# A conditional layer in 64x64 quarters whose tiles are turned by ScalarE's transposes, and products of zeros at both ends of an attention and feed-forward kernel

## The chip, the cores and the metric

The kernel runs on one core of one Trainium2 chip. The metric is the device time of one launch in microseconds (us), taken as the median of the runs shown. Below, PE is the matrix engine (TensorE), DVE the vector engine, ACT the scalar engine (ScalarE), POOL GpSimd, and SP the engine that issues most transfers. A phrase such as "L419" is line 419 of the kernel before.

## The reference

The input `x` has 64 batches of 64 channels and 1024 points in time. Two index vectors pick a weight set for each batch. Cut to what matters here:

```python
# x: (64, 64, 1024); itok_B_0_15: (64,) in 0..15; itok_B_0_7: (64,) in 0..7
W = weights[itok_B_0_15]                       # (64, 64, 64)
y = einsum('bct,bcd->bdt', x, W)               # the conditional layer
qkv = y @ attn_qkvw + attn_qkvb                # (.., 1024) @ (1024, 3072)
q, k, v = split into 32 heads of 32
probs = softmax(q @ k^T / sqrt(32))            # 64 x 64 per batch and head
x1 = x + (probs @ v) @ attn_ow + attn_ob
z = x1 @ W2^T + 2 * lora(x1, top-2 of 8 experts)
out = x1 + down(silu(gate(z)) * up(z))         # int8-quantized weights and activations
```

For every batch the conditional layer contracts over 64 channels with a 64x64 matrix of the batch's own. Its result has to stand with time on the partitions, because the projections to q, k and v contract over the 1024 points in time.

## The kernel before, in words

**Tiling.** Two batches of 64 channels make one tile of 128 rows and 1024 columns; there are 32 tiles, and four tiles are a block, so there are 8 blocks. In the attention stage (to about 1430 us) a block passes through four phases `c` = 0 to 3, one for every eight heads. All products of this stage are in f32.

**The conditional layer.** `load_x(b)` at the start of a block loads the four tiles of the next block (SP) and gathers their 64x64 weights (POOL). For each tile, the two weight matrices are copied into the diagonal blocks of a 128x128 matrix of zeros, `wbd` (L380, by POOL, in the first block by DVE). `conditional(b, tiles)` then makes eight products per tile with 128 columns of x as the stationary operand and `wbd` as the moving one (L355), which gives y with time on the partitions at once. Each half tile is copied out of PSUM by DVE (L361) or ACT (L363) into one of four quarters of the block, B11, B12, B21, B22 (rows by half of time, columns by half of the tokens; all are named yB in the profile). DVE makes four differences of quarters, T1 to T4 (L371, L376).

**Projections.** The projections use Winograd's scheme with seven products in place of eight, in the order 1, 6, 7, 5, 2, 4, 3. The first two use B11 and B22 and sums of them, the others T1 to T4. `rows_job` (L435) makes q or k of a phase: seven products of about 1.73 us; `values_job` (L462) makes v for two phases: seven of 3.45 us. After each product, its `rest` is run one product later: a copy by ACT (L406), a sum by DVE, or `put`, which writes a finished quarter: into `qT` for q, into `kbd` (keys with zeros between heads, four writes by ACT at L419 or by DVE at L421) for k, into `vbd` (L475) for v. The last two products of a job hold a PSUM bank of `ps_g` until they are put away, and the second product of the next job needs it.

**Scores, softmax, context.** `scores` (L498) multiplies q by kbd in 64x64 quadrants of PE, for two of four (half of heads, half of tokens) units at a time; a phase has two such groups, one at its start and one at its middle. DVE takes the maximum and subtracts it (L510, L511), ACT the exponential (L514), DVE the sum and the division (L520, L522). Then the probabilities are transposed without PE: ACT parts the f32 words into two int16 planes (`ph`, L528), SP issues a transposing transfer (`phT`, L533), and ACT joins the planes (`pT`, L540). `context` (L550) multiplies by vbd, ACT copies (L561) and issues the store of it (L562).

**The order of the work.** Nothing reorders the program: each engine works through its instructions in the order of emission. That order comes from a virtual clock. `run(cost, product, rest)` first calls everything whose due time in the list `due` has come, then emits a product, then the `rest` of the product before, and advances `now` by `cost`. `phase` puts the two score groups into `due` at 0 and at half of the phase's length, and hands the products in `fills` to `run`; each stage of softmax puts the next one into `due` with a fixed delay.

**The phases.** Phases 1 and 2 of a block hold q and k of the following phase. Phase 0 holds q, v for phases 2 and 3, and k. Phase 3 holds the whole conditional layer of the next block, then its v for phases 0 and 1, then its q and k. Phases 0 and 3 are the long ones. Phase 3 of the last block holds two products of the out-projection.

**Loads.** SP's queue carries x, the projections' weights (`wq`, `wk`: 1792 KB each, `wv`: seven of 512 KB), the transposes phT and some bfloat16 copies of later weights (`chores`), each at the place where it was emitted.

**The end.** The second stage (router, lora, quantized feed-forward) works through pairs of tiles. The end of its last pair is written out by hand: `gate_or_up` (L1491), `quant_b` (quantized rows transposed by a transfer or, with `by_pe`, by PE, L1481), and `down` (L1521), between DVE's work, which scales the results and finishes y (L1530).

Of the kernel before, what the change touches and what calls it, by code (L numbers as in the profile page):

```python
# [20 lines left out]
P = 128  # L21
# [161 lines left out]
def attention(tc, a, x_t, ctx_d, ident, dram, ps_g, KC, PB, NBLK, NCH, HPC, H, C, chores, early, op):  # L183
# [27 lines left out]
    with ExitStack() as ctx, ExitStack() as mid:  # L211
# [14 lines left out]
        xp = pool(early, "xp", 4)  # L226
# [12 lines left out]
        def load_x(b):  # L239
            tiles = []  # L240
            for j in range(PB):
                i = b * PB + j
                xt = xp.tile([P, H], F32, tag="x", name=f"x_{i}")
                if i == PB - 1:
                    held(xt[:, 0:1], tiles[0][0])
                nc.sync.dma_start(xt, x_t[i])
                wg = xp.tile([P, C], F32, tag="wg", name=f"wg_{i}")
                nc.gpsimd.indirect_dma_start(
                    out=wg[:, :],
                    out_offset=None,  # L250
                    in_=cw,
                    in_offset=bass.IndirectOffsetOnAxis(ap=idx[:, i:i + 1], axis=0),
                )
                tiles.append((xt, wg))
            return tiles

        def held(word, other):


            nc.scalar.copy(word, other[:, 0:1])  # L260
# [24 lines left out]
        def load_qk(b, wh, c, eng=None):  # L285
            t = w_qk[b, wh, c] = wp.tile([P, 7, KQ, P], F32, tag="wqk", name=f"w{wh}_{b}_{c}")
            if b == 0:
                if (wh, c) == ("q", 0):
                    held(t[:, SLOT["A11"], 0, 0:1], x_next[0][1])
                for key in RAW:  # L290
                    nc.sync.dma_start(t[:, SLOT[key], :, :], quarter(key, (0 if wh == "q" else H) + c * P, P))
                return sums(
                    eng or nc.vector, lambda key: t[:, SLOT[key], :, :], lambda: nc.gpsimd.dma_start(qk_d[wh, c], t)
                )
            nc.sync.dma_start(t, qk_d[wh, c])
# [21 lines left out]
        x_next = load_x(0)  # L317
# [7 lines left out]
        wbd = []  # L325
        for j in range(PB):
            t = w.tile([P, P], F32, tag=f"wbd{j}", name=f"wbd{j}")
            nc.vector.memset(t, 0.0)
            wbd.append(t)
# [12 lines left out]
        def conditional(b, tiles):  # L342

            def one(hf, j):
                key = f"B{hf + 1}{j // 2 + 1}"
                box = []

                def product():
                    xt = tiles[j][0]
                    if j % 2 == 0:  # L350
                        B[key] = yp.tile([P, KQ, HB], F32, tag=key, name=f"y{key}_{b}")
                    ps = ps_g.tile([P, 4, P], F32, tag="g", name=f"cond_{b}_{j}_{hf}")
                    for q in range(KQ):
                        k = hf * KQ + q
                        nc.tensor.matmul(ps[:, q, :], xt[:, k * P:(k + 1) * P], wbd[j], start=True, stop=True)  # L355
                    box.append(ps)

                def rest():
                    dst = B[key][:, :, (j % 2) * P:(j % 2 + 1) * P]
                    if j % 2 == 0:  # L360
                        nc.vector.tensor_copy(dst, box[0])  # L361
                    else:
                        nc.scalar.copy(dst, box[0])  # L363
                    if (hf, j) == (0, 3):
                        t_of("T1", "B12", "B11")
                    elif (hf, j) == (1, 3):
                        t_of("T2", "B22", "T1")
                        t_of("T3", "B22", "B12")
                    elif (hf, j) == (1, 1):
                        B["T4"] = B["B12"]  # L370
                        nc.vector.tensor_tensor(B["T4"], B["B21"], B["T2"], ALU.subtract)  # L371
                return 0.95, product, rest

            def t_of(key, x, y):
                B[key] = yp.tile([P, KQ, HB], F32, tag=key, name=f"{key}_{b}")
                nc.vector.tensor_tensor(B[key], B[x], B[y], ALU.subtract)  # L376

            for j, (_, wg) in enumerate(tiles):
                for r in range(2):
                    (nc.gpsimd if b else nc.vector).tensor_copy(wbd[j][halves[r], halves[r]], wg[halves[r], :])  # L380
            return [one(0, j) for j in range(PB)] + [one(1, j) for j in (2, 3, 0, 1)]
# [198 lines left out]
        def contexts(least=1):  # L580
            ready = sum(len(pTs) == 2 for *_, pTs in waiting)
            for n in range(ready if ready >= least else 0):
                context(*waiting.pop(0), 1.7 * n * (least - 1))

        def group(b, c, us):


            def begin():
                ps = scores(b, c, us)
                if behind:  # L590
                    behind.pop()()
                contexts(2)
                pTs = []
                waiting.append((b, c, us, pTs))
                for n, u in enumerate(us):
                    at(now + 1.7 * n, lambda n=n, u=u: first(u, ps[n], pTs))
                if b > 0:
                    at(now + 8.7, lambda: next(chores, None))
                    if c in (0, NP - 1):
                        at(now + 15, lambda: next(chores, None))  # L600
# [79 lines left out]
        for f in conditional(0, x_next):  # L680
            run(*f)
# [6 lines left out]
        for b in range(NBLK):  # L688
            if b + 1 < NBLK:
                x_next = load_x(b + 1)  # L690
            for c in range(NP):
                fills, length = [], None
                if c + 1 < NP:
                    fills += qk_fill(b, c + 1)
                    if c == 0:
                        fills[7:7] = v_fill(b, 1)
                        if b == 0:
                            for at_ in range(3, 7):
                                with_sums(fills, at_, v_raw, 1)
                elif b + 1 < NBLK:  # L700

                    fills += conditional(b + 1, x_next) + v_fill(b + 1, 0) + qk_fill(b + 1, 0)
# [305 lines left out]

class Winograd:
# [178 lines left out]
def second_stage(tc, a, out_t, xT_d, ident, ps_g, KC, NT, H, C, half, comb, op):  # L1188
# [12 lines left out]
    with ExitStack() as ctx:  # L1201
# [64 lines left out]

        ident_b = w.tile([P, P], BF16, tag="ident_b", name="ident_b")
# [200 lines left out]
        def quant_b(p, t, nm, by_pe=False):  # L1468
# [10 lines left out]
            ps = ps_g.tile([P, n // P, P], BF16, tag="g", name=f"qTp_{nm}_{p}_{t}")  # L1479
# [4 lines left out]
        def gate_or_up(p, t, nm):  # L1484
# [4 lines left out]
            ps = s["pgu", nm, t] = pool.tile([P, I], F32, tag=tag, name=f"p{nm}_{p}_{t}")  # L1489
            for k in range(KC):  # L1490
                nc.tensor.matmul(ps, qT[:, k, :], wt_b["w" + nm][:, k, :], start=(k == 0), stop=(k == KC - 1))  # L1491
# [22 lines left out]
        def down(p, t):  # L1514
            s = st[p]
            qT = s.pop(("qT", "i", t))
            for n in range(2):
                pool, tag = (ps_g, "g") if p == NPAIR - 1 else (ps_h, "h")
                ps = s["pd", t, n] = pool.tile([P, HH], F32, tag=tag, name=f"pd_{p}_{t}_{n}")
                for k in range(IC):  # L1520
# [136 lines left out]
        down(q, 0)  # L1657
# [5 lines left out]
        gate_or_up(p, 1, "g")  # L1663
        glu(p, 0)
        quant_b(q, 1, "i")
        gate_or_up(p, 1, "u")
# [8 lines left out]
        down(p, 0)  # L1675
        quant_b(p, 1, "i", True)
        result(q, 1, nc.gpsimd)
        result(p, 0, nc.gpsimd, nc.vector)
        down(p, 1)
# [55 lines left out]
```

## Time and profile before

| what | us |
|---|---|
| median of 3 runs | 2461.12 |
| lowest and highest run | 2460.36, 2464.75 |
| the profiled execution, its own time | 2458.5 |
| its span | 2456.7 |
| mean PE clock granted, of full speed | 0.998 |
| PE busy in the span | 2423.6 |
| DVE busy | 1532.9 |
| ACT busy | 953.2 |
| POOL busy | 362.9 |

The profile is one execution. Its time is the launch's, and the span runs from the first to the last instruction in the trace. "Busy" leaves out instructions that only wait, branch, or issue a transfer, so an engine can be held up for longer than its busy time says: the issue of a transposing transfer holds its engine too, and appears under SPq or ACTq, the sequencer of the engine. In a row of the timeline, the first number is the start and the second the length; what stands in brackets is the idle time before it and who ended it. In the waits, "A <- B: total, times, longest" says how long A's engine was idle until B's end released it.

### The profile page before, as it was taken

What the parts mean: (1) busy time and instruction counts of PE and PEld (TensorE: products, weight loads), DVE (VectorE), ACT (ScalarE), POOL (GpSimd) and SP (SyncE); (2) the same over time, 40 slices, a digit from 0 to 9 for tenths busy, and PEclk for the clock granted to TensorE, in tenths of its full rate; (3) what the DMA queues carried; (4) which work ended last, traced back from release to release, by engine and by line L of the source; (5) the groups of instructions that cost most, each with busy time, mean ns of one, the idle gap of its engine ahead of it and who ended that gap; (6) DMA issues with size and microseconds to landing.
All of it is one profiled execution on the core that took longest, in us unless ns stands there. A gap on an engine that the chain in (4) does not pass through costs nothing.

```text
span 2456.7 us, 34195 instructions
## 1 busy us (share of the span) xinstructions
PE 2423.6 (99%) x13194; PEld 1699.7 (69%) x13232; DVE 1532.9 (62%) x2955; ACT 953.2 (39%) x1304; POOL 362.9 (15%) x450
## 2 busy tenths in 40 slices
PE   8999999999999999999999999999999999999997
PEld 7888888888888888888888644444454545445452
DVE  4685585675664755745647633333367777878787
ACT  1343353342443443533434544344423333333333
POOL 5110001011122221210000243433200000000000
PEclk9999999999999999999999999999999999999999
DMA  8894767676677768766646588876744343434343
GB/s 275 286 268 150 219 198 234 189 213 211 199 204 248 202 193 249 206 204 180 176 142 218 175 266 247 268 239 218 235 140 80 88 80 77 89 70 92 74 118 75
DMA packets 419564, 448.07 MB, mean 182 GB/s; under 512 B 300737, under 2 KB 355010, under 8 KB 405698
## 3 DMA queue, kind: packets, MB, share of 16 engines
q1 hardware_dynamic: 388882, 379.21, 52.8%
q0 software_dynamic: 12080, 49.82, 7.6%
q10 hardware_dynamic: 18432, 16.79, 2.0%
q8 instruction: 106, 1.74, 0.3%
q14 instruction: 64, 0.52, 0.1%
HBM read 274.02 MB, written 100.66 MB: 153 GB/s over the span
## 4 chain that ended last, share of the span: by engine, by line
PE 95%; DVE 2%; ACT 1%; DMA 1%; issue 0%; ACTq 0%; SPq 0%; DVEq 0%
PE psva L462 5%; PE pska L435 5%; PE psvd L462 5%; PE psqa L435 5%; PE psvc L462 4%; PE psqc L435 4%; PE pskc L435 4%; PE psqd L435 4%; PE pskd L435 4%; PE pbc L1031 4%; PE pbd L1031 4%; PE pba L1031 4%; PE poa L1031 4%; PE pod L1031 4%; PE poc L1031 4%; PE s L498 3%
## 5 line engine op out<-in xcount | busy, mean ns | idle before, releaser
L540 ACT COPY pT<-phT 128x1024 int16<-128x1024 int16 x128 | 167.2, 1342 | 83.2 <-DMA phT<-ph 83.0
L514 ACT ACTIVATE prob<-prob 128x512 f32<-128x512 f32 x128 | 80.6, 630 | 258.6 <-DVE prob L511 232.4
L421 DVE SCALAR_TENSOR_TENSOR kbd<-pskd,bqkv,psku 32x256 f32<-32x256 f32 x256 | 123.2, 481 | 31.4 <-PE pskd L435 27.6
L528 ACT COPY ph<-prob 128x1024 int16<-128x1024 int16 x128 | 130.7, 1046 | 24.3 <-DVE prob L522 23.7
L1152 POOL TENSOR_TENSOR xo<-xo,ob 128x1024 f32<-128x1024 f32 x32 | 85.0, 2675 | 349.7 <-DVE To L1042 305.5
L561 ACT ACTIVATE co<-c,bqkv 128x256 f32<-128x256 f32 x128 | 60.1, 469 | 179.4 <-PE c L550 152.1
L435 PE MATMUL psqa<-yB,wq 128*128 128x256 f32 x512 | 123.6, 384 | 0.5 <-ACT psqp L406 0.5
L435 PE MATMUL pska<-yB,wk 128*128 128x256 f32 x512 | 122.6, 382 | 0.0
L1538 POOL DMA_DIRECT2D out_dram<-y x29 | 25.2, 869 | 656.2 <-DVE y L1530 644.4
L1126 ACT COPY xh<-xo 128x1024 int16<-128x1024 int16 x64 | 64.0, 1040 | 142.6 <-DVE xo L1171 142.6
L462 PE MATMUL psva<-wv,yB 128*128 128x256 f32 x512 | 117.1, 382 | 0.4
L1031 PE MATMUL poa<-woA,cx 128*128 128x512 f32 x256 | 115.4, 593 | 0.0
L1031 PE MATMUL pba<-wtA,x1T 128*128 128x512 f32 x240 | 107.9, 592 | 0.0
L1137 ACT COPY xTo<-xhT 128x1024 int16<-128x1024 int16 x64 | 84.6, 1338 | 58.4 <-DMA xhT<-xh 51.5
L435 PEld LDWEIGHTS pska<-yB,wk 128*128 128x128 f32 x512 | 96.0, 190 | 15.0 <-issue 2.4
L435 PEld LDWEIGHTS psqa<-yB,wq 128*128 128x128 f32 x512 | 95.1, 190 | 16.0 <-issue 2.8
L462 PEld LDWEIGHTS psva<-wv,yB 128*128 128x128 f32 x512 | 96.1, 190 | 14.4 <-ACT yB L363 1.2
L510 DVE TENSOR_REDUCE mx<-s 128x8 f32<-128x512 f32 x128 | 87.7, 685 | 10.7 <-PE s L498 9.3
L511 DVE TENSOR_TENSOR prob<-s,mx 128x512 f32<-128x512 f32 x128 | 88.5, 691 | 9.3 <-DVE mx L510 0.5
L520 DVE TENSOR_REDUCE den<-prob 128x8 f32<-128x512 f32 x128 | 86.7, 678 | 7.7 <-ACT prob L514 6.9
L522 DVE TENSOR_TENSOR prob<-prob,den 128x512 f32<-128x512 f32 x128 | 88.6, 692 | 4.4
L1031 PEld LDWEIGHTS poa<-woA,cx 128*128 128x128 f32 x256 | 48.4, 190 | 60.1 <-issue 59.7
(251 smaller groups left out, 5140.1 us busy)
## 6 DMA issues: line engine op xcount, KB each, us to landing
wv<-v_d SPq DMA_DIRECT2D x98, 512.0 KB, 4.0
wq<-q_d SPq DMA_DIRECT2D x28, 1792.0 KB, 7.6
wk<-k_d SPq DMA_DIRECT2D x28, 1792.0 KB, 8.1
x<-in_x_dram SPq DMA_DIRECT2D x32, 512.0 KB, 9.2
ctx_d<-co ACTq DMA_DIRECT2D x128, 128.0 KB, 3.9
cx<-ctx_d SPq DMA_DIRECT2D x16, 1024.0 KB, 6.9
xo<-in_x_dram SPq DMA_DIRECT2D x32, 512.0 KB, 5.6
xT_d<-xTo SPq DMA_DIRECT2D x64, 256.0 KB, 3.3
```

What stands on the lines that cost most here:

```text
L421: nc.vector.scalar_tensor_tensor(dst, ps, bias, u, ALU.add, ALU.add)
L435: nc.tensor.matmul(ps[:, 0:HB], A[:, SLOT[A_OF[i]], k, :], B[B_OF[i]][:, k, :], start=first and k == 0, stop=k == KQ - 1, skip_group_check ...
L462: nc.tensor.matmul(ps[:, j * VC:(j + 1) * VC], B[B_OF[i]][:, k, j * P:(j + 1) * P], A[:, k, :], start=first and j == 0 and k == 0, stop=k ...
L510: nc.vector.tensor_reduce(mx_v, ps, AX.X, ALU.max)
L511: nc.vector.tensor_tensor(p.rearrange("p (a e) k -> p a e k", a=2), ps, mx_v.unsqueeze(3).to_broadcast([P, 2, HPC, C]), ALU.subtract)
L520: nc.vector.tensor_reduce(den, p, AX.X, ALU.add)
L522: nc.vector.tensor_tensor(p, p, den.unsqueeze(2).to_broadcast([P, n, C]), ALU.mult)
L528: nc.scalar.copy(h, planes(p.rearrange("p n k -> p (n k)")))
L540: nc.scalar.copy(planes(pT.rearrange("p a b q -> p (a b q)")), hT)
L1031: self.nc.tensor.matmul(ps, self.B[self.B_OF[i]][:, k, :], self.A[self.A_OF[i]][:, k, :], start=first and k == 0, stop=k == self.KQ - 1, s ...
L1137: nc.scalar.copy(planes(xT.rearrange("p k q -> p (k q)")), hT)
L1152: nc.gpsimd.tensor_add(s["x"][:, t, :], s["x"][:, t, :], self.ob)
```

## The change

The conditional layer of blocks 1 to 7 is no longer made with block-diagonal weights in phase 3. `conditional_tile(b, j)` makes one tile with four products, each on another 64x64 quadrant of PE: the 64x64 weights are stationary and 512 columns of x are moving. The result has channels on the partitions, in the two PSUM buffers `ps_c` that the context products also use. ACT parts it into int16 planes (`parted_y`, two copies per tile), ACT issues the transposing transfers (`turned_y`, two per tile), and ACT joins the planes into the quarters (`joined_y`: one copy for the first half of time, two for the second), at due times after the tile's product.

The tiles are spread. Of block b+2, tile 0 is made in phase 3 of block b after the fourth product of v, tile 1 in the same phase between q and k; tile 2 in phase 0 of block b+1 at its first score group, and tile 3 in that phase between v and k. The four tiles of block 1 are made in phase 0 of block 0: after q, at the second group of scores of phase 0, between v and k, and at the first score group of phase 2. The quarters have two sets, for even and odd blocks. T1 to T4 are made one at a time at the last two products of phase 2 and the first two of phase 3. x is loaded tile by tile: when tile j is made, the load of the tile after the next one is issued. Phase 3 holds v, q and k of the next block and no conditional stage.

The first block keeps its products; its four wbd matrices are one tile of memory, cleared by one operation. 22 products of bfloat16 zeros (128x512) are issued ahead of its first product, and 30 more in seven places of the last pair of the second stage.

The diff, cut to its core:

```diff
@@ conditional layer @@
-        def conditional(b, tiles):
+        def quarter_of(b, key):
+            return (yp if b % 2 else w).tile(
+                [P, KQ, HB], F32, tag=key if b % 2 else key + "e", name=f"y{key}_{b}"
+            )
...
+        T_OF = (("T1", "B12", "B11"), ("T2", "B22", "T1"), ("T3", "B22", "B12"), ("T4", "B21", "T2"))
+        def conditional():
...
+                    if (hf, j) == (0, 0):
+                        idle_products(nc, zero, ps.rearrange("p q t -> p (q t)"), 22)
...
-                    (nc.gpsimd if b else nc.vector).tensor_copy(wbd[j][halves[r], halves[r]], wg[halves[r], :])
+                    nc.vector.tensor_copy(wbd[halves[r], j, halves[r]], x_of[0, j][1][halves[r], :])
...
+        def conditional_tile(b, j):
+            xt, wg = x_of.pop((b, j))
+            ps = [ps_c.tile([P, 2, HB], F32, tag="c", name=f"cond{hf}_{b}_{j}") for hf in range(2)]
+            for hf in range(2):
+                for r in range(2):
+                    nc.tensor.matmul(
+                        ps[hf][halves[r ^ hf], :, :], wg[halves[r], :], xt[halves[r], hf * 512:(hf + 1) * 512],
+                        start=True, stop=True,
+                    )
+            if j + 2 < PB:
+                load_x(b, j + 2)
+            elif b + 1 < NBLK:
+                load_x(b + 1, j + 2 - PB)
+            def parted_y(hf):
+                h = w.tile([P, 2, 512], I16, tag="yh", name=f"yh_{b}_{j}_{hf}", bufs=2)
+                nc.scalar.copy(h, planes(ps[hf].rearrange("p a t -> p (a t)")))
...
+            def turned_y(hf):
...
+                hT = w.tile([P, 2, 512], I16, tag="yhT", name=f"yhT_{b}_{j}_{hf}")
+                nc.scalar.dma_start(
+                    hT.rearrange("p h (k q) -> p (h k) q", q=P), h.rearrange("p h t -> p (h t)"), transpose=True
+                )
...
+            def joined_y(hf):
...
+                for r in range(2) if hf else (slice(0, P),):
...
+                    nc.scalar.copy(dst, src[:, :, :, halves[r] if hf else r])
+            for time, f, hf in (
+                (1.7, parted_y, 0), (3.4, parted_y, 1), (3.5, turned_y, 0), (8.5, joined_y, 0), (8.6, turned_y, 1),
+                (13.6, joined_y, 1),
+            ):
+                at(now + time, lambda f=f, hf=hf: f(hf))
+        tile_groups = [(0, 0, 2), (0, 2, 0)] + [(b, 0, 0) for b in range(1, NBLK - 1)]
@@ group @@
-                contexts(2)
+                if not contexts(2) and (b, c, us[0]) in tile_groups:
+                    next_tile()
@@ phases @@
+                        for n in (14,) if b else (14, 7):
+                            fills[n:n] = [(0.9, next_tile, None)]
+                    if c + 2 == NP and b + 1 < NBLK:
+                        sums_to_come = [lambda b=b, n=n, Y=Y: t_of(b + 1, Y, *T_OF[n]) for n in range(4)]
+                        with_sums(fills, -2, sums_to_come, 1)
+                        with_sums(fills, -1, sums_to_come, 1)
...
-                    fills += conditional(b + 1, x_next) + v_fill(b + 1, 0) + qk_fill(b + 1, 0)
+                    fills += v_fill(b + 1, 0) + qk_fill(b + 1, 0)
+                    with_sums(fills, 0, sums_to_come, 1)
+                    with_sums(fills, 1, sums_to_come, 1)
...
+                    if b + 2 < NBLK:
+                        tiles_to_come += [(b + 2, j) for j in range(PB)]
+                        for n in (14, 4):
+                            fills[n:n] = [(0.9, next_tile, None)]
@@ idle products @@
+def idle_products(nc, zero, ps, count):
+    for _ in range(count):
+        nc.tensor.matmul(ps, zero[:, 0:P], zero, start=True, stop=True, skip_group_check=True)
...
-        down(q, 0)
+        down(q, 0, 6)
...
-        gate_or_up(p, 1, "g")
+        gate_or_up(p, 1, "g", 5)
...
-        gate_or_up(p, 1, "u")
+        gate_or_up(p, 1, "u", 6)
...
-        down(p, 0)
-        quant_b(p, 1, "i", True)
+        down(p, 0, 3)
+        quant_b(p, 1, "i", True, 8)
...
-        down(p, 1)
+        down(p, 1, 2)
```

## The prediction before the run

> **What bounds the kernel now.** I read four views in this order: the share of busy time with the chain that ended last, the waits of PE, the timelines of PE, ScalarE and SP around one conditional stage, and the windows at both ends. First the page's busy row and the chain's row of engines.
>
> ```profile
> PE 2423.6 (99%) x13194; PEld 1699.7 (69%) x13232; DVE 1532.9 (62%) x2955; ACT 953.2 (39%) x1304; POOL 362.9 (15%) x450
> PE 95%; DVE 2%; ACT 1%; DMA 1%; issue 0%; ACTq 0%; SPq 0%; DVEq 0%
> ```
>
> PE works from 9 us to the end with 33 us idle in all. So there are two ways to move the time: take work off PE, or make PE wait where it does not wait now. ScalarE at 39% looks free, but that is a mean over stages. PE's waits, the longest three:
>
> ```profile
> PE cond L355 <- DVE wbd L380: 9.2, 1, 9.2
> PE qTp_i L1481 <- DVE qb_i L1474: 2.0, 1, 2.0
> PE pd L1521 <- DMA qT_i<-qb_i: 1.9, 1, 1.9
> ```
>
> The first is the start, the others lie in the last 50 us. In the attention stage, after the start, PE never waits over 0.7 us: what ScalarE delivers there arrives in time, and the question is by how much. Now PE's timeline around the conditional layer of one block (start, length, engine, line, operation, tiles, count).
>
> ```profile
> 518.93 1.10 PE L498 MATMUL s<-kbd,qT 64*64 64x128 f32 x32
> 519.96 2.08 PE L550 MATMUL c<-pT,vbd 128*64 128x64 f32 x64
> 521.98 7.41 PE L355 MATMUL cond<-wbd,x 128*128 128x128 f32 x64
> 529.22 3.62 PE L462 MATMUL psva<-wv,yB 128*128 128x256 f32 x16
> ```
>
> The reader is to see that a block's conditional layer holds PE from 521.98 to 529.22, 7.24 us, and that one group of scores, with four 64x64 quadrants of the array at work side by side, takes 519.96 - 518.93 = 1.03 us.
>
> **The change part by part: what PE gets rid of.** In blocks 1 to 7 the products with block-diagonal weights (half of each array multiplies zeros) become four products per tile, one on each 64x64 quadrant, 64 weights wide and 512 columns long. A tile streams 4 x 512 columns in four passes of f32: 8192 column passes. A score group (16 products of 128 columns, four passes) streams 8192 as well, in 1.03 us. A block's four tiles then cost 4.12 us, a gain of 7.24 - 4.12 = 3.12 us; 7 blocks: **-21.8 us**. The bounds: with no overhead 0.85 us per tile, -26.9 us; two quadrants at a time 1.7 us per tile, -3; one after the other 3.4 us, a loss. The score row speaks for 1.03.
>
> **What moves to other engines.** Per tile ScalarE now parts (2 copies like ph, 1.05 us), issues 2 transposes, and joins (one copy like pT, 1.34 us, and two half ones, 0.72 each): 4.9 us. 28 tiles add 137 us, less its 28 old evictions of 0.59 (L363): 953 becomes about 1074 us busy, 44%, and the issues hold it besides. DVE loses 28 evictions of 0.68 (L361), POOL its 56 copies into wbd of 0.23. The differences T1 to T4 (four operations of 1.22 us per block) move from the conditional stage to the end of phase 2 and the start of phase 3. From 500 to 518, the end of such a phase 2, DVE worked 13.82 of 18 us, so two of them fit: I cost all of this at nothing, since it hides beside PE; without that cover each T would be late by its own 1.22 us, once or twice per block. Loads of x go out one tile at a time (32 before and after) and one tile ahead: 9.2 us to landing, against over 20 us between tiles. Nothing; if the weight loads before them on SP's queue held them up, the tile would wait for the rest of the landing.
>
> **What is added to the path.** ScalarE's queue is in order, and it also makes kbd, the keys that the next phase's second score group needs. Two rows show when.
>
> ```profile
> 407.47 1.91 ACT L419 ACTIVATE kbd<-pska,bqkv 32x256 f32<-32x256 f32 x4 [5.29 <-PE pska L435]
> 410.81 1.10 PE L498 MATMUL s<-kbd,qT 64*64 64x128 f32 x32
> ```
>
> kbd is done at 409.38 and is read at 410.81: 1.43 us to spare. What the change puts ahead of kbd on ScalarE can only eat that before PE stops. Next, the transposes. By the dependences of the built program, ScalarE's transposes (yhT) and SP's (phT, of the softmax) never overlap: each waits until the last one of the other engine has landed. [...] What one costs shows on SP and on ScalarE:
>
> ```profile
> 452.06 1.23 SPq L533 DMA_TRANSPOSE phT<-ph  x1
> 456.32 1.35 ACT L540 COPY pT<-phT 128x1024 int16<-128x1024 int16 x1 [2.57 <-DMA phT<-ph]
> DMA to landing us min/median/max: 3.0/3.6/7.3
> ```
>
> An issue holds its engine for 1.23 us and the landing follows 3.6 us after its start (4.26 here). On ScalarE a transpose has no row; its copies issue in 0.33 us. I take SP's 1.23, the row of the same kind; the other end is 0.33.
>
> *Tile between q and k of phase 3* (T = 0 when PE starts the tile). PE is done with it at 1.0, with k's first product at 2.8. ScalarE: pskp until 3.3, second parted copy until 4.35, first yhT issued 4.35 to 5.6, landing at 7.95; pT of the third softmax quarter meanwhile. SP's fourth phT waits for 7.95 and lands at 11.65. ScalarE: its pT until 13.1, first join until 14.4, second yhT (which waited for that phT) until 15.65, kbd until 17.6. PE ends k's seven products at 13.2 and can start the scores' second half at 13.75. Stall: 17.6 - 13.75 = **3.8 us**, where 1.4 were to spare. Six such tiles, and block 0's between v and k, which I count alike: +26.6 us.
>
> *Tile between v and k of phase 0.* SP's third phT is issued at 0.6, behind the last load of v, and lands at 4.9 (the 4.26 of above). Only then the first yhT, 4.9 to 6.15, landing at 8.5; SP's fourth phT lands at 12.2; second yhT until 13.5, kbd 15.4: a stall of **1.7 us**, six times: +10.2 us.
>
> *The other two tiles* (after the fourth v product of phase 3, and at phase 0's first group) have no kbd close behind them: the same walk leaves 0.6 us and more. Nothing; with a landing of 4.3 it would be 0.8 us six times.
>
> Behind the waiting ScalarE stand exponentials, whose softmax feeds SP's next transposes; DVE waits for them, and PE only for context products a group later. Costed at nothing beyond the stalls.
>
> [...]
>
> **Both ends.** At the start 22 products of zeros run before x arrives. The windows (us, PE busy, PE clock granted, DMA share, GB/s):
>
> ```profile
> 9.22:14.20 4.98, 4.98 (x23) 1.00 0.84 247
> 14.20:19.07 4.87, 4.87 (x43) 1.00 1.14 302
> ```
>
> PE finishes 23 products in the first five microseconds and 43 in the next: half rate, although the clock column says 1.00. [...] DVE delivers the fourth wbd at 12.71, so the stage can end at 17.3 and not 19.07: **-1.7 us**. I take the counts. At the tail:
>
> ```profile
> 2440.00:2444.00 4.00, 1.43 (x9) 1.00 0.00 0
> 2444.00:2448.00 4.00, 2.74 (x8) 0.62 0.98 177
> ```
>
> The last down product runs at 0.62, 2.74 us for 1.73. The 30 idle products fill gaps that are 0.7 to 2.0 us long with 0.4 to 1.7 us each, so they fit. But behind that product the end is DVE's and a store's, and DVE is busy without a gap: 0 (-1.0 to +0.5).
>
> **Sum.** -21.8 + 26.6 + 10.2 - 1.7 = +13.3 us. The profiled execution took 2458.5 us around a span of 2456.7 (1.8 outside); with the change 2471.8. The median of the runs is 2461.1, 2.6 above the profiled one, so the median forecast is 2474.
>
> **The rivals.** A measurement of this kernel can tell about 0.2%, 5 us, from no change.
> - A, faster: landings of 2.7 us (the value of the kernel's other transposes, xhT) and an issue of 0.33. The first walk then leaves a stall of 1.1 us x 7 = 7.7, the second 0: -21.8 - 1.7 + 7.7 = -15.8, 2445 us. For it: xhT's row; nothing else loads SP in phase 3. Against: phT's own median, beside weight loads. If the transposes turned out not to wait for each other, the same side, 2437. Chance 0.27. It turns at stalls of 23.5 us in all, 1.8 per tile of the thirteen.
> - B, the same: landings of 3.0, phT's minimum: 2.6 x 7 + 0.5 x 6 = 21.2; -2.3, 2459 us. Chance 0.13.
> - C, the sum above: slower, 2474, own range 2466 to 2482. Chance 0.45.
> - D, much slower: landings of 4.3 throughout: (5.2 x 7) + (3.1 x 6) + (0.8 x 6) = 60; +36.5, 2498 us. Or the quadrants run only two at a time and the tiles give nothing: +32. For it: the transposes of ScalarE fall among loads of 1792 KB. Chance 0.15.
> - That the change would not do what it says is excluded for the products, which stand in the built order; for the start it would mean 1.7 us, inside the range.
>
> **How the numbers follow.** Likeliest is C, 2474. Faster 0.27 (A); within 0.2% 0.13 (B); slower 0.60 (C and D). The range from 2445 (A's value; about 0.13 below it) to 2495 (just short of D's value; under 0.1 above it) holds 8 in 10.
>
> **What would show it.** Right: a wait of PE for kbd that is new, some thirteen times, 2 to 4 us each; PE's idle time up by about 35 us and its busy time down by about 22; ScalarE waiting for phT and yhT; 1.0 us per tile in PE's timeline; the first products at full rate and the first stage over by 17.5; the tail as before. Wrong: no such wait (A), or waits for yB or T at the start of a phase, which I cost at nothing; or tiles of 1.7 us and more.

## The result and the profile after

| | before | after |
|---|---|---|
| median, us (6 runs each) | 2461.38 | 2554.60 |
| lowest and highest, us | 2460.36, 2464.75 | 2544.76, 2571.81 |
| span of the profiled execution, us | 2456.7 | 2555.7 |
| PE busy, us | 2423.6 | 2453.4 |
| mean PE clock granted | 0.998 | 0.981 |

The changed kernel is slower: the ratio of the times is 1.0385, with an interval from 1.0367 to 1.0404. That is 93 us, seven times what was forecast. First the busy row of the page after.

```profile
PE 2453.4 (96%) x13021; PEld 1673.7 (65%) x13060; DVE 1512.9 (59%) x2925; ACT 1062.2 (42%) x1416; POOL 347.1 (14%) x395
```

The reader is to see two things. PE is idle for 102 us where it was idle for 33. And it is busy for 30 us more, although its products have become cheaper. Of these, 15.0 us are the 52 products of zeros; and the clock in the table is lower, where the same products take longer (28.4 us from 20 to 1560 us, below). PE's longest waits (total, times, longest):

```profile
PE s L564 <- ACT kbd L485: 46.7, 25, 12.6
PE cond L401 <- ACT yh L412: 17.3, 1, 17.3
PE psqa L501 <- ACT psqp L472: 10.0, 3, 5.6
PE pska L501 <- ACT pskp L472: 4.3, 2, 3.4
PE c L616 <- ACT pT L606: 4.1, 1, 4.1
```

All five are waits for ScalarE; the one for kbd is the one forecast. Where they lie shows when the run is cut at the first score group of each block. Length of each block in us, from one such group to the next, read from PE's timelines (block 7 keeps its length up to its last score group, so it is left out):

| block | 0 | 1 | 2 | 3 | 4 | 5 | 6 | sum |
|---|---|---|---|---|---|---|---|---|
| before | 171.7 | 170.9 | 170.1 | 170.1 | 170.7 | 170.4 | 170.7 | 1194.5 |
| after | 213.7 | 176.2 | 178.0 | 187.5 | 185.4 | 176.3 | 171.8 | 1288.9 |

Block 0 alone loses 42 us, blocks 1 to 6 together 52. The start gains 1.9 us, and from block 7's late score group to the end 6.5 us more are lost.

**One stall.** The tile between q and k at the end of block 1, ahead of block 2's first scores, on PE (start, length, engine, line, operation, tiles, count, idle before):

```profile
443.00 1.09 PE L401 MATMUL cond<-x,wg 64*64 64x512 f32 x8
...
456.30 0.67 PE L564 MATMUL s<-kbd,qT 64*64 64x128 f32 x16
462.54 0.69 PE L564 MATMUL s<-kbd,qT 64*64 64x128 f32 x2 [5.57 <-ACT kbd L485]
...
466.27 2.50 PE L501 MATMUL psqa<-yB,wq 128*128 128x256 f32 x8
```

The tile takes 1.02 us (443.00 to 444.02), as forecast. Thirteen microseconds later PE waits 5.57 us for kbd. The same stretch on ScalarE and its sequencer, and on SP:

```profile
446.11 1.36 ACTq L420 DMA_TRANSPOSE yhT<-yh  x1
...
457.69 1.33 ACT L606 COPY pT<-phT 128x1024 int16<-128x1024 int16 x1 [8.82 <-DMA phT<-ph]
458.89 1.32 ACT L434 COPY yB<-yhT 128x1024 int16<-128x1024 int16 x1
460.24 1.26 ACTq L420 DMA_TRANSPOSE yhT<-yh  x1
461.55 1.91 ACT L485 ACTIVATE kbd<-pska,bqkv 32x256 f32<-32x256 f32 x4 [1.34 <-issue]
452.62 1.24 SPq L599 DMA_TRANSPOSE phT<-ph  x1
```

And SP's second longest wait over the whole run:

```profile
SPq L599 <- DMA yhT<-yh: 253.7, 40, 13.3
```

These are the steps of the forecast's walk, in its order: the first yhT is issued 3.1 us after the tile's start (forecast 4.35); SP's phT, which waits for it (SP waits for yhT 40 times in the run, 253.7 us), goes out only at 452.62; pT, join, second transpose and kbd follow one another. Their lengths differ: the first yhT lands 6.5 us after its issue and phT 5.1 us after its own, where the walk has 3.6 and 3.7. What the walk did not have at all is the next view: the same stretch in windows (us, PE busy, PE clock, DMA share, GB/s).

```profile
456.00:458.00 2.00, 0.97 (x18) 1.00 0.67 206
...
460.00:462.00 2.00, 0.00 (x0) 0.62 1.06 452
462.00:464.00 2.00, 1.17 (x11) 0.50 1.16 308
...
466.00:468.00 2.00, 2.00 (x9) 0.67 0.22 72
468.00:470.00 2.00, 2.00 (x11) 1.00 0.56 190
```

In this stall the clock falls to half 3.5 us into the idle time (460.5) and comes back after 4.7 us of work (467.5). A stall that is followed by such a dip costs its idle time and then, over the twelve dips of the run, 1.5 to 3.1 us more, with 3.0 to 6.2 us of work in the dip. Summed over all windows of 2 us from 20 to 1560 us (busy time times what is missing of the clock), before loses 0.0 us to a low clock and after 28.4, in 12 dips; idle time in the same stretch is 3.4 and 84.7. Of the 28.4 us, 14 belong to the six stalls at the start of phase 0, 6 to block 0, 6 to two stalls in blocks 3 and 4, and 3 to block 7.

**Block 0.** ScalarE, while v's first weights are summed, stored and read back:

```profile
81.83 1.36 ACTq L420 DMA_TRANSPOSE yhT<-yh  x1
...
101.90 1.34 ACT L434 COPY yB<-yhT 128x1024 int16<-128x1024 int16 x1 [14.44 <-DMA yhT<-yh]
103.27 1.31 ACTq L420 DMA_TRANSPOSE yhT<-yh  x1
121.64 1.38 ACT L434 COPY yB<-yhT 128x512 int16<-128x512 int16 x2 [18.40 <-DMA yhT<-yh]
```

Each of the first tile's two transposes takes some 18 to 20 us from issue to join, and ScalarE stands in front of it with everything behind: PE idles 17.3 us for yh, then 3.4 for pskp and 12.6 for kbd. What makes these two transposes so late is not shown; loads on SP are in flight beside them.

**Blocks 3 and 4.** A tile between v and k; its second transpose lands 14 us after the issue, among SP's loads. First ScalarE, then PE:

```profile
697.11 1.25 ACTq L420 DMA_TRANSPOSE yhT<-yh  x1
711.45 1.38 ACT L434 COPY yB<-yhT 128x512 int16<-128x512 int16 x2 [8.28 <-DMA yhT<-yh]
713.77 3.78 PE L501 MATMUL psqa<-yB,wq 128*128 128x256 f32 x8 [5.63 <-ACT psqp L472]
```

The copy psqp stands behind that join. PE idles 5.63 us, and its next product takes 3.78 us where 1.89 is usual. This is not the same in every execution: a run below that leaves these two blocks as they are (block 0's tiles elsewhere) has them at 180.1 and 180.5 us in place of 187.5 and 185.4.

### The profile page after: what moved, and what is told of

Same layout as the page of the kernel before. It is cut to its first block, busy times and chain, and to the rows that moved or that the text cites. A ratio compares the mean times of both kernels' runs of the same rounds, so it can differ in the third digit from the quotient of the medians.

```text
span 2555.7 us, 33981 instructions
## 1 busy us (share of the span) xinstructions
PE 2453.4 (96%) x13021; PEld 1673.7 (65%) x13060; DVE 1512.9 (59%) x2925; ACT 1062.2 (42%) x1416; POOL 347.1 (14%) x395
## 4 chain that ended last, share of the span: by engine, by line
PE 65%; DMA 5%; ACT 2%; DVE 1%; issue 1%; ACTq 0%; SPq 0%; DVEq 0%
PE pbc L1124 4%; PE pba L1124 4%; PE pbd L1124 4%; PE poa L1124 4%; PE pod L1124 4%; PE poc L1124 4%; DMA yhT<-yh 3%; PE psqa L501 2%; PE pr L1395 2%; PE psqd L501 2%; PE psqc L501 2%; PE psva L528 2%; PE pska L501 2%; PE pu L1589 2%; PE pg L1589 2%; PE psvd L528 2%
## 5 line engine op out<-in xcount | busy, mean ns | idle before, releaser
L501 PE MATMUL psqa<-yB,wq 128*128 128x256 f32 x512 | 131.1, 401 | 10.0 <-ACT psqp L472 10.0
L564 PE MATMUL s<-kbd,qT 64*64 64x128 f32 x2048 | 83.9, 285 | 46.8 <-ACT kbd L485 46.7
L434 ACT COPY yB<-yhT 128x512 int16<-128x512 int16 (+1 forms) x84 | 76.2, 951 | 94.8 <-DMA yhT<-yh 94.7
L564 PEld LDWEIGHTS s<-kbd,qT 64*64 64x64 f32 x2048 | 60.1, 137 | 75.7 <-ACT kbd L485 54.0
```

The costliest lines, as they stand in the source:

```text
L501: nc.tensor.matmul(ps[:, 0:HB], A[:, SLOT[A_OF[i]], k, :], B[B_OF[i]][:, k, :], start=first and k == 0, stop=k == KQ - 1, skip_group_check ...
L564: nc.tensor.matmul(ps[halves[r], hp, n, jj * 2:(jj + 1) * 2, :], q_of[b, c][halves[hp], m, t * HB + t0:t * HB + t0 + C], kbd[u][halves[hp] ...
```

## The experiments

**The tiles' transposes from SP's queue.** Then no transpose waits for another engine's.

```diff
@@ turned_y @@
-                nc.scalar.dma_start(
+                nc.sync.dma_start(
```

> The transposes of the tiles (yhT) are issued by SP in place of ScalarE, at the same places of the program; all transposes then stand in one queue and none waits for another engine's. Theory 1 (the two engines' transposes wait for each other, and kbd, behind them on ScalarE, comes late): the waits of PE for kbd fall from 46.7 us in all to under 10, the dips of the PE clock go with them, and block 0 loses most of its extra 42 us: 2440 to 2470 us. Rival A (the added transposes simply land late because the DMA engines are loaded): a few per mille either way, 2530 to 2560. Rival B (ScalarE has too much to copy): no change, 2540 to 2570.

Measured: 2465.74 us (before, beside it: 2457.19), ratio 1.0036 (1.0024 to 1.0047). Its waits of PE:

```profile
PE s L564 <- ACT kbd L485: 5.5, 10, 1.6
PE cond L401 <- ACT yh L412: 5.0, 1, 5.0
```

The wait for kbd falls from 46.7 to 5.5 us, block 0 to 181.7 us, the dips from 12 to 3. Of 93 us, some 85 go with one word. But the edit removes two things at once: the waits between the engines, and the issues and landings of ScalarE's transposes.

**No transposes at all.** `turned_y` hands the parted planes on, so y is left unturned and the result is not the layer's.

```diff
@@ turned_y @@
-                h = hs[hf]
-                hT = w.tile([P, 2, 512], I16, tag="yhT", name=f"yhT_{b}_{j}_{hf}")
-                nc.scalar.dma_start(
-                    hT.rearrange("p h (k q) -> p (h k) q", q=P), h.rearrange("p h t -> p (h t)"), transpose=True
-                )
-                hTs[hf] = hT
+                hTs[hf] = hs[hf]
```

> The transposes of the tiles are left out: the joining copies read the parted planes directly, all copies of ScalarE stay. Theory 1 and rival A: stalls for kbd and dips of the clock go, and what is left is the gain of the cheaper products and of the ends, 22 + 3 us: 2430 to 2445 us. Rival B (ScalarE's copies are too much): stalls stay, over 2500.

Measured: 2442.24 us, ratio 0.9941 (0.9924 to 0.9957). Blocks 0 to 6 sum to 1173.4 us, 21.1 less than before: this is the gain of the products. ScalarE's copies hold up nobody, nor does anything else that the change moved (the sums T1 to T4, the loads of x): PE idles 4.6 us from 20 to 1560 us. The time is 5 us above the band's middle, since this kernel too loses 5.5 us in block 7 (below).

**kbd ahead of the join and the second transpose**, waits between engines kept.

```diff
+            a, b_, c_ = (10.0, 10.1, 15.1) if b > 1 and j in (1, 3) else (8.5, 8.6, 13.6)
...
-                (1.7, parted_y, 0), (3.4, parted_y, 1), (3.5, turned_y, 0), (8.5, joined_y, 0), (8.6, turned_y, 1),
-                (13.6, joined_y, 1),
+                (1.7, parted_y, 0), (3.4, parted_y, 1), (3.5, turned_y, 0), (a, joined_y, 0), (b_, turned_y, 1),
+                (c_, joined_y, 1),
```

> For tiles 1 and 3 of blocks 2 to 7, the first joining copy and the second transpose come after kbd in ScalarE's queue (due times 10.0, 10.1 and 15.1 for 8.5, 8.6 and 13.6); the transposes and their waits stay. Theory 1 with the queue as its means: kbd no longer waits for a landing and for an issue, the stalls of about 4 us at the start of phase 0 fall below 1.5, and with them six dips of the clock of 3.3 us each: about 45 us less, 2505 to 2520; block 0 keeps its 42. Rival A (late landings hold PE by another way): under 15 us less. Rival B: no change, as the same copies are made.

Measured: 2537.95 us, ratio 1.0340 (1.0321 to 1.0360): about 11 us less by the ratios, where 45 were expected. PE's waits show why:

```profile
PE s L565 <- ACT kbd L486: 22.8, 12, 11.7
PE psvb L529 <- ACT qT L486: 22.4, 4, 7.2
```

The wait for kbd halves, and of what is left 11.7 us is block 0's. In its place comes a wait for qT, which now stands behind the second join: the lateness is passed on, with new dips of the clock. Here the order on ScalarE decided who waits more than how much is late: PE's idle time from 20 to 1560 us is 78.6 where it was 84.7.

**Zeros where PE waits for kbd.**

```diff
@@ scores @@
...
+                if (n, c, us[0]) == (1, 0, 0) and 0 < b < NBLK - 1:
+                    for _ in range(30):
+                        nc.tensor.matmul(
+                            ps[:, 0, 1, :, :], kept[:, 0:P], kept, start=True, stop=True, skip_group_check=True
+                        )
```

> In phase 0 of blocks 1 to 6, 30 bfloat16 products of zeros (128x256, about 0.11 us each, 3.2 in all) stand between the two halves of the first score group, where PE waits for kbd. Nothing else changes, kbd comes as late as before. Theory 2 (after about 3 us idle PE's clock is halved for some 6.5 us of work, which costs 3.3 us per stall): the six stalls shrink to about 1 us each of idle time, the clock stays at 1.00 there, and the time falls by 6 x 3.3 = 20 us, to 2530 to 2540. Rival (the low clock is a throttle with a cause of its own, such as power): 2550 to 2560, the dips stay.

Measured: 2544.93 us, ratio 1.0353 (1.0336 to 1.0370), 0.3% below the changed kernel and not 0.8%. The windows around block 3's stall, where PE then still idled 2.2 us:

```profile
644.00:646.00 2.00, 0.33 (x3) 1.00 0.86 301
646.00:648.00 2.00, 1.46 (x23) 1.00 1.12 368
648.00:650.00 2.00, 2.00 (x12) 1.00 1.23 120
```

At five of the six places the clock stays at 1.00, so the dips follow from the idle time. Time lost to a low clock falls from 28.4 to 12.6 us over the stage. How much of that comes back as time is not settled: the median falls by some 8 us and the two intervals touch, and the profiled executions differ where the edit changes nothing (block 0 takes 218.9 us and not 213.7). Small new waits for psqp (0.9 and 1.1 us in block 3) and for qT (0.9, 1.8 and 0.6 us late in blocks 3 to 5) take a part of it.

**Block 0's tiles elsewhere**, with ScalarE's transposes: one between v and k of phase 0, two among phase 1's products, one at phase 2's first group.

```diff
-        tile_groups = [(0, 0, 2), (0, 2, 0)] + [(b, 0, 0) for b in range(1, NBLK - 1)]
+        tile_groups = [(0, 2, 0)] + [(b, 0, 0) for b in range(1, NBLK - 1)]
...
-                        for n in (14,) if b else (14, 7):
+                        for n in (14,) if b else (14,):
...
+                    for n in {(0, 1): (8,1)}.get((b, c), ()):
+                        fills[n:n] = [(0.9, next_tile, None)]
```

> The changed kernel, ScalarE's transposes included, but the four tiles made in block 0 stand elsewhere: one between v and k of phase 0, two among the products of phase 1 (after the first and the eighth), one at the first score group of phase 2. None is made while the first weights of v are still written and read back. Theory 1 with that place as the reason for block 0's 42 us: block 0 costs under 15 us more than before, and the time falls by 25 to 35 us, to 2515 to 2530. Rival A (every tile of block 0 meets a full DMA): the stalls move with the tiles, 2545 to 2555.

Measured: 2525.74 us, ratio 1.0283 (1.0244 to 1.0323). Block 0 takes 192.2 us in place of 213.7 (215.7 and 218.9 in the two runs before this one, which leave these tiles in place); the 20.5 us it still loses are more than the 15 allowed for. Half of block 0's cost was the place.

**Both ends alone**, in the kernel before: the lines of the change with `idle_products` are added to it, with the zeros that they read, and no others.

> The kernel before with the products of zeros at both ends alone: 22 ahead of the first product, 30 in the last pair of the second stage. The forecast's terms were -1.7 for the start and 0 (-1.0 to +0.5) for the tail: 1 to 3 us less than before, and the first score group at 66.5 us in place of 68.2. If the clock column of 1.00 at the start was right, no difference.

Measured: 2458.86 against 2460.00 us, ratio 0.9993 (0.9985 to 1.0002), which doesn't tell it from no change. In its trace the first q product starts at 17.15 us and not at 19.07, and from block 7's last score group to the end it takes 1.6 us less. Block 5 hides both in this execution: 174.9 us for 170.4, where PE's context products came in pieces with gaps of 0.2 to 0.5 us, 1.9 us in all, and the clock was halved after them.

**All transposes of the long phases on ScalarE**: the softmax's transposes of phases 0 and 3 join the tiles' there.

```diff
@@ turned @@
-            nc.sync.dma_start(
+            (nc.scalar if c in (0, NP - 1) and b < NBLK - 1 else nc.sync).dma_start(
```

> The changed kernel with the softmax's transposes (phT) of phases 0 and 3, blocks 0 to 6, issued by ScalarE too; the tiles' transposes stay on ScalarE, and only at the border to phases 1 and 2 do the two engines' transposes still wait for each other. ScalarE gets 56 more issues of about 1.25 us. It parts the two costs that moving the tiles' transposes to SP removed together. If the waits between the engines are what costs: nearly as good as that run, 2465 to 2490. If ScalarE's own issues and its order are what costs: no better than the changed kernel, 2545 or more.

Measured: 2511.29 us, ratio 1.0210 (1.0184 to 1.0236), between the two expectations. By the ratios, ending the waits between the engines inside the long phases is worth some 43 us, net of the 56 more issues that ScalarE gets; and 43 more separate it from SP's queue, 22 of them in block 0, which stays at 203.6. Landings, ScalarE's own issues and the waits left at the border to phases 1 and 2 can each have a part in these, and no run separates them. One row shows a late landing, with ScalarE's transpose ahead of block 4's first scores and SP's load beside it:

```profile
777.96 1.36 ACTq L420 DMA_TRANSPOSE yhT<-yh  x1
790.06 1.33 ACT L434 COPY yB<-yhT 128x1024 int16<-128x1024 int16 x1 [8.17 <-DMA yhT<-yh]
774.94 0.32 SPq L297 DMA_DIRECT2D wq<-q_d  x1
```

12.1 us from issue to join, with no transpose of SP in the way, behind a load of 1792 KB (and smaller ones).

**That load 9.5 us later.**

```diff
@@ rows_job, done @@
-                    next_load()
+                    if wh == "q" and c == 0 and b > 0:
+                        at(now + 9.5, next_load)
+                    else:
+                        next_load()
```

> The run with all of the long phases' transposes on ScalarE, and the load of q's weights (wq, 1792 KB) that SP issues just before the tile between q and k now comes 9.5 us later. There the tile's first transpose landed 12 us after its issue, and no transpose of SP was in its way. If it lands late because the load's pieces fill the DMA engines: the landings fall to 4 to 6 us, the stalls for kbd (18 us in all) fall below 8 and the time by 10 to 25 us, to 2485 to 2500. If a transpose of ScalarE is slow by itself: no change, 2505 to 2520.

Measured: 2505.89 us beside a before of 2457.40, ratio 1.0211 (1.0191 to 1.0232): no change. The move worked in two of the blocks only. In block 2 the load now goes out 3.9 us after the transpose:

```profile
434.64 1.32 ACTq L420 DMA_TRANSPOSE yhT<-yh  x1
439.14 1.34 ACT L434 COPY yB<-yhT 128x1024 int16<-128x1024 int16 x1 [0.59 <-DMA yhT<-yh]
438.51 0.42 SPq L297 DMA_DIRECT2D wq<-q_d  x1
```

The join follows after 4.5 us, where the run before had 8.6, and the block's first part takes 28.1 us and not 36.5. In blocks 4 and 5 other loads stood ahead of it on SP, it went out 0.2 us before the transpose, and the joins took 12.7 and 11.4 us, with stalls of 5.5 and 4.3. Over the six places of this run, the join comes 4.5 and 5.2 us after the issue where the load goes out behind the transpose, and 7.3 to 12.7 us where it goes out ahead of it. So landings follow the loads in flight in these rows, but the time of the run doesn't show it: ahead of block 1 the load still went out first, and PE waited 3.0 us where it had waited 0.6.

**SP's queue and kbd first**: the edits of the first and the third experiment together.

> Both repairs at once: the transposes of the tiles issued by SP, and for tiles 1 and 3 of blocks 2 to 7 the first join after kbd. Theory 1: the waits for kbd left in the run with SP's transposes (5.5 us, one with a dip of the clock) go: 2456 to 2463 where the kernel before takes 2457; block 0 keeps its 10 us. If something else on ScalarE becomes late (qT or the copies of the first product), as in the run with kbd first: no gain over the 2465 of SP's transposes alone.

Measured: 2454.62 against 2460.00 us, ratio 0.9978 (0.9970 to 0.9986): the quarters now win, by 5 us. Blocks 1, 2, 4 and 5 take 167.7 to 167.9 us, block 0 still 182.2.

**The same with block 0's tiles moved, four ways.** First between v and k of phase 0, after the third and the tenth product of phase 1, and at the first group of phase 2 (the edit of the moved tiles above with 10 and 3 for 8 and 1; with ScalarE's transposes a program with these places deadlocks, so they have no time there):

> As the run before, with block 0's four tiles moved as in the first run of this set. Theory 1: block 0 loses its 10 us as well and every block keeps 2.5 us of the 3.1 that the products save: 2445 to 2455, faster than the kernel before. If phase 1's ScalarE has no room for two tiles: the stalls turn up there for qT and kbd, 2460 or more.

Measured: 2457.65 us, ratio 0.9991 (0.9984 to 0.9998). That lies between the two expectations. Phase 0 is nearly back at its old pace (52.0 us for 50.8), but phase 2 waits for kbd, qT and pskp (5.0, 2.0, 4.0 us), and block 0 takes 187.1. Then two in phase 0 and one in each of the next two, with kbd first for block 1's second tile too and block 7's contexts moved:

```diff
-                        for n in (14,) if b else (14, 7):
+                        for n in (14,) if b else (14,):
...
+                    for n in {(0, 1): (7,)}.get((b, c), ()):
+                        fills[n:n] = [(0.9, next_tile, None)]
...
-                    at(now + 20, contexts)
+                    at(now + 23.5, contexts)
```

> SP's transposes and kbd first (also for block 1's second tile), with block 0's first tile taken out from behind q, where ScalarE waited 17 us for its transpose: block 0's tiles at the second score group of phase 0, between v and k, in the middle of phase 1 and at the first group of phase 2. And the last contexts of block 7 stand one product of the out-projection later, where PE waited 2.6 to 4.2 us for pT. Theory 1: block 0 loses most of its 11 us, the late stall its 3 to 5: 2440 to 2447 where the kernel before takes 2460. If the first tile's wait was only passed on: 2450 to 2455.

Measured: 2454.08 us, ratio 0.9974 (0.9964 to 0.9983). Block 0 takes 180.7, but the moved contexts make PE wait 2.1 and 4.1 us for pT, and the time is that of the second expectation. Third, one in phase 0, one in phase 1 and two in phase 2, by `{(0, 1): (10,), (0, 2): (4,)}`, contexts moved as well, and kbd first for block 1's first tile in place of its second:

> As the run before, but block 0's tiles stand between v and k of phase 0, after the tenth product of phase 1, at the first group of phase 2 and after that phase's fourth product. Theory 1: phase 0 keeps the pace of before, and if ScalarE has room for two tiles in phase 2, 2438 to 2445; if not, qT and kbd come late there as in the run with two tiles in phase 1, and it takes 2450 to 2458.

Measured: 2468.10 us, ratio 1.0032 (1.0020 to 1.0044), slower than either expectation, block 0 at 192.1: phase 2 waits 5.3 us for yh, and the scores after it 5.7 for kbd. With two tiles of 4.9 us of ScalarE each, this short phase takes 42.6 us where it took 29.4. Last, the second way with the contexts back in place (`now + 20`):

> The run with SP's transposes, kbd first and block 0's tiles from the second score group on, with the contexts of block 7 at their old place: there the later place had put both groups' contexts together and PE waited 2.1 and 4.1 us for pT. That wait shrinks to the 2.5 us of the other runs: 2449 to 2453 where the kernel before takes 2460.5. If the two places cost the same: 2454.

Measured: 2451.88 against 2457.40 us, ratio 0.9975 (0.9964 to 0.9986). By the intervals that is no different from the second way or from leaving block 0's tiles where they were. In block 7 PE waited 4.0 us for pT in the old place too.

## Why the prediction was wrong, point by point

The mechanism that the prediction walked through, kbd late on ScalarE behind transposes that wait for each other, came true, and with about the stalls that it entered: 33.0 us for the twelve tiles outside block 0, where 31.8 were measured. What failed are three terms that it put at nothing or nearly so: the clock after a stall (28.4 us), block 0 (42 us where one stall of 3.8 was entered), and late landings of ScalarE's transposes with what stands behind them (waits for psqp of 9.5 us in blocks 3 and 4). They overlap, since part of the 28.4 us lies in the other two.

- *The products* (-21.8): right. Without transposes the seven blocks gain 21.1. The four passes that the forecast counts for f32 are no rows of a trace; what before shows is times, four times as long per column: 4 x 256 columns of f32 take 1.73 us (psqc, 24.98 to 26.71), 8 x 512 of bfloat16 1.74 us (pu, 2434.60 to 2436.34).
- *The start* (-1.7): right in the trace (1.9), within the noise by the time of the whole run. The counts were the row to believe there, not the clock column. That the first stage ends 4.6 us after the fourth wbd was the author's estimate, and no run shows that term by itself; what the runs showed is q's first product at 17.17 us in the changed kernel, at 17.15 and 17.28 in the run with the load later and in the last one, and not at 19.07. But it is no sure gain: in 11 of the 14 traces with these zeros, the first real product came 0.5 to 1.5 us after the last zero and q's first product at 17.0 to 17.4 us; in the other three the gap was 2.0 to 2.2 us, and q's came at 18.6 to 19.1.
- *The tail* (0, -1.0 to +0.5): right for the changed kernel. From the end of the out-projection on, the changed kernel takes 0.2 us more; the kernel with both ends alone takes 1.4 us less there in its trace, just outside that range.
- *Tile between q and k* (3.8 us of stall): right in kind, and near in size with some luck. Blocks 0 to 5 make six such tiles, and the waits at the next phase are 3.0, 5.6, 4.4, 5.0, 4.1 and 2.9 us, mean 4.2. In the stall shown the landings were 4.3 us longer than in the walk, the first issue 1.2 us earlier, and PE went on before kbd's last write (462.54 against 463.46), which the walk waits for.
- *Tile between v and k* (1.7): right in kind, 0.5 to 1.6 us, but two of its late joins held up psqp in blocks 3 and 4 (the third term below).
- *The term that failed first*: "The clock of PE stays at 1.00 after a stall" was never written down, but each stall was entered at its idle time alone. All six stalls of 2.9 us and more at phase 0 halved the clock. Measured in the changed kernel: 28.4 us; the zeros in the gaps showed that the dips come from idling, and what they would save in time is open. The prediction's own windows have PE at half rate after 9.2 us of idle time at the start (23 products in 4.98 us, then 43 in 4.87); this was not carried over to the stalls that the same sum put into the middle of the run, where the traces show the half clock from stalls of 2.9 us on.
- *The second*: "block 0's between v and k, which I count alike" and nothing for its other three tiles. Block 0 lost 42 us, the largest single miss: 36 of idle time and 6 of low clock. The landing of 3.6 us was SP's, mostly in steady blocks; the first tile's two transposes there took 18 and 20 us to be joined.
- *The third*: "costed at nothing beyond the stalls" for what stands behind the waiting ScalarE, with a landing that is the same wherever it is issued. Of ScalarE's landings the trace gives 22 of 56, with a median of 4.2 us and up to 14.3; of SP's in the same run 32 of 128, with 3.2 and up to 5.4. Joins 14.3 and 12.6 us after the issue cost blocks 3 and 4 waits for psqp of 5.6 and 3.9 us and two dips.
- *Late in block 7*: 6.5 us, which no step had: PE waits 4.1 us for pT where it waited 0.6, and 3.0 us go to the half clock behind it. Every kernel with quarters lost 2 to 7 us there, the one without transposes too, mostly around such a wait. Why pT comes late there is not settled.

The sum, from rows: idle time from 20 to 1560 us +81.3, low clock +28.4, products -21.1, start -1.9, together 86.7 of the span's 99.0. The other 12 us have no row of their own. They come to about 1 us for each stall, where the scores trickle in behind kbd's four writes and count as busy (0.9 us from 462.54 to 463.46 in the stall shown); for the rest of the stalls that is argued, not shown.

Of the rivals, the change of side was priced at 1.8 us per tile. As far as the runs part them, the waits between the engines decided about half: ended inside the long phases, with the transposes on ScalarE, they give back some 43 of 93 us, and that kernel is still 2.1% slower than before. So a gain of 23.5 us without the waits, A's 2437, finds no support there. With them on SP, which ends the waits and frees ScalarE, the kernel is within 0.4% of before, and with kbd moved ahead 0.2% faster. D named landings as the danger and put 4.3 us on them throughout; that was near ScalarE's median (4.2), and the tail above it, with block 0, was what cost.

## What to carry to other kernels

A stall on a full PE had two prices here: the idle time, and the slower clock after it, 1.5 to 3.1 us in each of the twelve dips; enter both for stalls like those that halved the clock here, 2.9 us and more. The transposes of the two engines became one chain through their waits (SP waited 253.7 us for yhT); put such transposes into one queue, and choose its engine by what else stands behind the waiting issue: here SP's queue gave back 85 us, ScalarE's (in the long phases) 43. When an engine gets new work ahead of what the bottleneck waits for, move the latter ahead of it, and check who is then behind it: alone that mostly passed the lateness on (some 11 us less, where 45 were expected), and it brought the kernel below before only once the waits were gone (2454.62 against 2460.00 us).

## What the runs showed of the hardware that was not expected

- Idle times of 2.9 us and more at phase 0 halved PE's clock: the six of the changed kernel (2.9 to 5.6 us) and those of 3.0, 5.5 and 4.3 us in the run with the load later. Shorter ones sometimes did: the 1.6 us and 0.5 us of block 4 with SP's transposes did, 1.8 us in block 3 of the same run did not. Five gaps of 0.2 to 0.5 us, 1.9 us within some 3 us, did too (block 5 with both ends alone).
- Zeros ahead of the first product did not always bring q's first product forward: after a gap of up to 1.5 us it came at 17.0 to 17.4 us, after 2.0 to 2.2 us at 18.6 to 19.1 (19.07 before).
- Where a transpose is issued changed the tail of its landing and hardly the middle. Of the landings that the traces give, the tiles' transposes took 4.2 us in the median and up to 14.3 from ScalarE (22 of 56), 4.3 and up to 9.8 from SP (27 of 56). In the run with kbd first and moved tiles on SP that was best (2451.88), 5.3 and up to 8.3 (34 of 56). Block 0's 18 and 20 us from ScalarE are not among the 22; counted to the join, the longest is 20.1 us from ScalarE and 9.8 from SP.
